# A two-layer decoder on one core: the first layer's feed-forward split by batch pairs, its weights and scratch moved, its heads made by pairs

## The chip, the cores and the metric

The kernel runs as one program on 1 core of one Trainium2 chip. The metric is device time in microseconds (us), lower is better. The time before is the median of 3 runs, 899.75 us, with 895.15 and 903.39 us as the ends. One more execution was taken by the hardware profiler; all durations below come from it.

## What is computed

The input is x of 4 batches by 256 tokens by 256 features and a context of 4 by 256 by 128. Two pre-norm decoder layers follow. Cut to what matters:

```python
x = x + L0_attn(ln(x))            # 8 query heads and 2 key/value heads of 32, rotary, unit layernorm
                                  # of q, k, v; window of 64 tokens; tanh soft cap; softmax
x = x + L0_xattn(ctx, ln(x))      # state-space scan of the context, 256 channels x 16 states,
                                  # its output gated by silu(ln(x))
x = x + L0_ffn(ln(x))             # silu(x@gate.T*gs) * (x@up.T*us) @ down.T * ds, 704 wide
x = x + L1_attn(ln(x))            # 16 query and 4 key/value heads of 128, causal
x = x + L1_xattn(ctx, ln(x))      # a second scan, gated in the same way
x = x + L1_ffn(ln(x))             # 32 experts, 6 chosen per token, and a shared expert
```

The scan is `state = state * exp(d * A) + d * u * B`, `y = sum over states of state * C`, along the 256 tokens. It depends on the context alone; only the gate at its end needs x.

## The kernel before

Tokens lie on the 128 partitions, so x is eight tiles of 128 tokens, two per batch. All arithmetic on TensorE is 32-bit except the far-mask product (L486); each 32-bit product is recorded as two instructions.

**The scan.** A scan is run for a pair of batches at a time (bp 0 or 1, two batches side by side in a row of 512). `mamba_front(l, bp, ...)` makes u, dt and du on TensorE, ScalarE and VectorE and writes the rows of B and C to DRAM (L204). `mamba_scan` is a Python generator. Each state costs: two row loads `bt` and `ct` on SyncE's queue (L232), an exponential on ScalarE into a PSUM bank (L238), `db` on GpSimd (L240), the scan instruction on VectorE (L241) and the product with ct on VectorE (L243). In layer 0 every second state is added up on TensorE (L258) and the others on GpSimd (L260), and one `next` of the generator makes two states; a pair of batches has 32 states, that is 16 steps (2 channel halves of 8). In layer 1 a step is one state number for both halves, added up on GpSimd (L250).

**Layer-0 attention.** `head0(b)` makes the normalized, rotated heads of one batch: projections (L393), rotation (L403, L409, L410), mean and square sum (L417 to L426), an inverse square root by three Newton steps in `rsqrt_steps` (L105 to L112), and the scaled heads (L433 to L440). `tail0(b, ..., states)` does scores, tanh, exp, the weighted sum and the output projection, and calls `states(2)` at two places, so that scan steps are traced between its parts.

**The order of the work.** The program is traced in Python in the order in which it is written; a scheduler then fills each engine's queue by that order as priority and by when it expects operands, buffers and PSUM banks to be free. On the chip each queue runs in order. The traced order around the change is: heads of batches 0 and 1; then for b = 0 to 3: two scan steps, head0(b+2) if there is one, tail0(b) with two and two more steps. After b = 0 the front of the second scan is traced, and the 3 MB weight `wqkv1` of layer 1 is loaded behind the last row load (L576). So 24 of the 32 steps are traced with the attention.

**Layer-0 feed-forward** comes next, in a `with` block of its own (L614 to L679): its weights downs, gw, uw and dw are loaded there (L618 to L624), into a pool that opens when the attention's pools have closed, and dw is scaled on GpSimd (L625). For each half hf (batches 0 and 1, then 2 and 3): the gates `gates_of` (L275), in the second half the rest of the scan (`states(99)`), `mamba_gate` (L286 to L294) and `ln_transposed` (L137 to L144) of each batch, all through the single PSUM bank of `pc`; then six pieces of 128 columns: gate and up products (L643), silu (L651), product (L654); then the down product (L669) and the sum into x (L677). In the second half five steps of layer 1's first scan are traced between the pieces. `mamba_front(1, hf, pf)` is traced after each half.

Before that block the mean over each head's 128 columns is taken out of wqkv1, in four groups of five heads: a reduction on VectorE (L607, L608) and two subtractions on GpSimd (L610). Layer 1's attention (from L683) opens its PSUM pools after `stage_a.close()` has given back all of layer 0's.

Two buffers matter: `tile_pool` PSUM banks are pa=1, pb=2, pc=1, psd=2, psy=1, pf=1, all eight; and ScalarE runs Silu, Softplus and Exp/Tanh with different function tables, each change being an ACT_TABLE_LOAD in the trace.

## Time and profile before

| what | value |
|---|---|
| median of 3 runs | 899.75 us (895.15 to 903.39) |
| the profiled execution | 899.26 us, of which the span is 897.5 us |
| TensorE clock granted, mean | 0.941 |
| busy share of the span | PE 90%, VectorE 66%, ScalarE 54%, GpSimd 47% |
| batch sums of layer-0 attention into x (L551) | at 95.3, 132.5, 157.5 and 185.6 us |
| last scan state of layer 0 added up (second L262 of bp 1) | 252.4 us |
| first product of layer 1 (L714) | 317.6 us |
| first expert product on the chain (L1015) | 650.6 us |

The span is 1.8 us shorter than the profiled execution's own time, and that is 0.5 us under the median. The stretches used below are: 0 to 132 us (heads, attention of batches 0 and 1), 132 to 186 (attention of batches 2 and 3), 186 to 253 (feed-forward of batches 0 and 1 beside the last 16 states), 253 to 317 (gates and feed-forward of batches 2 and 3), then layer 1.

In a list of groups the columns are line, engine, operation, output and inputs, shapes, count, then busy us and mean ns of one, then the idle time just before them and what ended it. In a table of stretches each engine has its busy us and its instruction count, then come the granted clock and the DMA share. In the chain of waits a row is start, length and what.

### The profile page before, as it was taken

The page shows a single profiled execution, that of the slowest core. Times are in us where ns is not written, and L with a number is a line of the kernel's source. Part 1 is how long each engine was busy: PE and PEld are TensorE (multiplying, and loading weights), DVE is VectorE, ACT ScalarE, POOL GpSimd, SP SyncE. Part 2 cuts the span into 40 slices and gives each one's busy share as a digit, 9 for nine tenths or more (in the row PEclk, how much of TensorE's full clock was granted, in tenths as well). Part 3 has the DMA queues.
Part 4 walks back from the last instruction along what each step waited for, and adds up shares of the span by engine and source line. Part 5 has one row for each costly group of instructions (what it writes and reads, how often), then busy time and mean ns, then how long its engine had stood idle before and what let it go on. Part 6 is the DMA issues. An engine that isn't in the chain of part 4 may idle for free.

```text
span 897.5 us, 10261 instructions
## 1 busy us (share of the span) xinstructions
PE 803.8 (90%) x3062; PEld 496.9 (55%) x3062; DVE 588.2 (66%) x1112; ACT 480.7 (54%) x1188; POOL 423.2 (47%) x427
## 2 busy tenths in 40 slices
PE   5788989978978989889898978997999999999997
PEld 2345656623433435546565745675666656666665
DVE  4897999775877668777759785788067676212121
ACT  5565545478848736746856693776333433211111
POOL 5654879865779624735635472422257751000000
PEclk9896889778986999999999999998999999999999
DMA  5545465672623400100110010000048743555542
GB/s 165 174 144 212 148 181 195 196 257 76 206 93 102 147 15 24 39 10 30 41 47 24 24 47 1 24 3 21 29 153 225 233 151 101 150 148 159 158 145 82
DMA packets 61015, 98.36 MB, mean 110 GB/s; under 512 B 6352, under 2 KB 26720, under 8 KB 60704
## 3 DMA queue, kind: packets, MB, share of 16 engines
q1 hardware_dynamic: 60080, 96.48, 34.4%
q10 hardware_dynamic: 880, 1.23, 0.4%
q8 instruction: 24, 0.39, 0.2%
q14 instruction: 31, 0.25, 0.1%
HBM read 96.24 MB, written 1.44 MB: 109 GB/s over the span
## 4 chain that ended last, share of the span: by engine, by line
PE 46%; DVE 12%; ACT 5%; POOL 3%; issue 3%; POOLq 0%; DVEq 0%; ACTq 0%
PE ps L1015 13%; PE ps L1029 12%; PE ps L883 5%; PE ps L714 4%; PE ps L868 2%; PE ps L821 2%; DVE ps L741 2%; DVE qs L734 1%; ACT sc L840 1%; DVE qr L742 1%; PE ps L748 1%; DVE h L241 1%; PE ps L669 1%; PE ps L643 1%; POOL sc L845 1%
## 5 line engine op out<-in xcount | busy, mean ns | idle before, releaser
L240 POOL TENSOR_TENSOR db<-bt,du 128x512 f32<-128x512 f32 x128 | 162.7, 1282 | 82.2 <-DVE h L241 57.0
L241 DVE TENSOR_TENSOR_SCAN h<-h,db 128x512 f32<-128x512 f32 x128 | 152.7, 1215 | 29.2 <-ACT h L238 28.1
L1015 PE MATMUL ps<-moe_xnT,w 128*128 128x512 f32 x272 | 128.9, 597 | 0.0
L1029 PE MATMUL ps<-w,hT 128*128 128x256 f32 x544 | 128.5, 379 | 0.0
L1020 DVE SCALAR_TENSOR_TENSOR hT<-ps,gr 128x512 f32<-128x512 f32 x64 | 44.1, 689 | 126.8 <-PE ps L1015 126.8
L238 ACT ACTIVATE h<-dt,negA 128x512 f32<-128x512 f32 x128 | 86.2, 689 | 73.5 <-DVE hc L243 71.2
L1029 PEld LDWEIGHTS ps<-w,hT 128*128 128x128 f32 x544 | 103.0, 190 | 40.2 <-issue 29.4
L1021 ACT ACTIVATE hT<-hT 128x512 f32<-128x512 f32 x68 | 42.8, 629 | 133.8 <-DVE hT L1020 133.6
L714 PE MATMUL ps<-wqkv,xnT 128*128 128x512 f32 x192 | 93.4, 598 | 8.0 <-DVE rq L706 5.6
L243 DVE TENSOR_TENSOR hc<-h,ct 128x512 f32<-128x512 f32 x128 | 84.8, 678 | 3.0 <-DMA ct<-bc 1.8
L250 POOL TENSOR_TENSOR y<-y,hc 128x512 f32<-128x512 f32 x64 | 80.8, 1272 | 8.3 <-DVE hc L243 6.4
L845 POOL TENSOR_TENSOR sc<-sc,rsum 128x512 f32<-128x512 f32 (+1 forms) x32 | 46.2, 1466 | 66.4 <-DVE rsum L843 66.3
L1015 PEld LDWEIGHTS ps<-moe_xnT,w 128*128 128x128 f32 x272 | 51.9, 192 | 36.5 <-issue 33.2
L707 POOL TENSOR_TENSOR rq<-rq,nhalf 128x8 f32<-128x8 f32 x20 | 33.0, 1651 | 80.9 <-DVE rq L706 80.7
L729 ACT ACTIVATE sq<-ps 128x128 f32<-128x128 f32 x160 | 42.4, 282 | 49.4 <-PE ps L714 49.4
L840 ACT ACTIVATE sc<-sc,nm 128x256 f32<-128x256 f32 (+1 forms) x128 | 56.7, 448 | 7.6 <-DVE nm L835 4.2
L883 PE MATMUL ps<-wo,oT 128*128 128x256 f32 x256 | 57.0, 381 | 0.0
L883 PEld LDWEIGHTS ps<-wo,oT 128*128 128x128 f32 x256 | 48.1, 190 | 8.9 <-ACT oT L876 2.6
L714 PEld LDWEIGHTS ps<-wqkv,xnT 128*128 128x128 f32 x192 | 32.7, 190 | 30.1 <-issue 17.5
L258 PE MATMUL ps<-hc,ident 128*128 128x512 f32 x64 | 39.9, 712 | 8.8 <-DVE hc L243 8.8
L260 POOL TENSOR_TENSOR y<-y,hc 128x512 f32<-128x512 f32 x32 | 40.8, 1274 | 4.8 <-DVE rs_t L110 2.1
L748 PE MATMUL ps<-ident,qr 128*128 128x128 f32 x160 | 28.1, 293 | 13.7 <-DVE qr L742 11.8
(206 smaller groups left out, 1450.6 us busy)
## 6 DMA issues: line engine op xcount, KB each, us to landing
bt<-bc SPq DMA_DIRECT2D x96, 256.0 KB, 3.5
ct<-bc SPq DMA_DIRECT2D x96, 256.0 KB, 3.8
w<-in_w_dram SPq DMA_DIRECT2D x64, 256.0 KB, 3.7
gr<-gt SPq DMA_DIRECT2D x64, 256.0 KB, 3.4
wqkv<-in_wqkv_dram SPq DMA_DIRECT2D x1, 3072.0 KB, 11.8
wo<-in_wo_dram SPq DMA_DIRECT2D x1, 2048.0 KB, 9.3
x<-in_x_dram SPq DMA_DIRECT2D x4, 256.0 KB, 5.1
w<-in_ws_dram SPq DMA_DIRECT2D x4, 256.0 KB, 3.9
```

What stands on the lines that cost most here:

```text
L238: nc.scalar.activation(h, dt[:, c, :], AF.Exp, scale=negA[:, a : a + 1])
L240: nc.gpsimd.tensor_mul(db, bt, du[:, c, :])
L241: nc.vector.tensor_tensor_scan(h, h, db, 0.0, ALU.mult, ALU.add)
L243: nc.vector.tensor_mul(hc, h, ct)
L250: nc.gpsimd.tensor_add(y[:, c, :], y[:, c, :], state(n, c, bt, ct))
L714: mm(pq, lhsT=xnT[:, f, c * P : (c + 1) * P], rhs=wqkv1[:, f, ch * 512 : (ch + 1) * 512], start=(f == 0), stop=(f == 1),)
L840: nc.scalar.activation(part, part, AF.Exp, bias=nm[:, qc, j : j + 1], accum_out=rsum[:, qc, j : j + 1])
L845: nc.gpsimd.tensor_mul(part, part, rsum[:, qc, :].unsqueeze(2).to_broadcast([P, 4, w]))
L883: mm(pout[:, c * 256 : (c + 1) * 256], lhsT=oTs[h // 4][:, h % 4, c * P : (c + 1) * P], rhs=wo1[:, 8 * gp + h, :], start=(h == 0), stop=(h ...
L1015: mm(ph_, lhsT=w[:, f * P : (f + 1) * P], rhs=xnT[:, f, :], start=(f == 0), stop=(f == 1))
L1020: gated.append(nc.vector.scalar_tensor_tensor(h, ph_, 0.0, g, ALU.max, ALU.mult).ins)
L1029: mm(po[t // 2][:, (t % 2) * 256 : (t % 2 + 1) * 256], lhsT=h[:, t * P : (t + 1) * P], rhs=w[:, 256:512], start=start and t % 2 == 0, stop ...
```

## The change

1. **Feed-forward as a generator.** `feed_forward(hf, room, pair, narrow)` holds the same work as before, with a `yield` after the gates, after each batch's gate and norm, after each of six pieces and after each down product: 11 pieces. `pair` and `narrow` say which PSUM banks it takes.
2. **Batches 0 and 1 beside the attention of batches 2 and 3.** Its pieces are traced two at a time with three scan steps (`both`), before each of the two batches and at the two fill places of each tail0. It takes the banks pf and pa in turn, and its scratch (sz, xnT, hT, sg) is the memory of wqkv1.
3. **Weights.** The feed-forward's weights get a pool that stands beside the attention's, and are loaded after batch 0, where wqkv1 was loaded; wqkv1 is loaded after the first half of the feed-forward has ended, as it shares the memory.
4. **Scan steps.** 2 + 3 + 3 for each of batches 0 and 1, then steps until the first scan has ended (17 in all), then `both`. The front of layer 1's first scan and conv_taps(1) are traced inside this stage.
5. **Heads by pairs.** `head0` does two batches up to the inverse square root in one set of instructions of double width; `normed(i)` makes the scaled heads of one. Some tiles go from two buffers to one.
6. **rsqrt_steps** has three instructions per Newton step, not four, everywhere.
7. **Second half.** Its narrow products go through pc and pa in turn; its gates are made at its start; the centring of wqkv1 (`centre`) is traced between its pieces, and the front of layer 1's second scan after the third pair.

```diff
         for _ in range(3):
-            nc.vector.tensor_mul(t_, r_, r_)
+            nc.vector.scalar_tensor_tensor(t_, r_, -0.5, r_, ALU.mult, ALU.mult)
             nc.vector.tensor_mul(t_, t_, v)
-            nc.vector.tensor_scalar(t_, t_, -0.5, 1.5, ALU.mult, ALU.add)
-            nc.vector.tensor_mul(r_, r_, t_)
+            nc.vector.scalar_tensor_tensor(r_, t_, 1.5, r_, ALU.add, ALU.mult)
...
+    fw = stage_a.enter_context(tc.tile_pool(name="f0w", bufs=1))
...
+    def load_ffn():
+        nc.sync.dma_start(out=downs, in_=rows[:, R_DOWNS : R_DOWNS + HID].to_broadcast([P, HID]))
+        nc.sync.dma_start(out=gw, in_=gate_in)
+        nc.sync.dma_start(out=uw, in_=up_in)
+        nc.sync.dma_start(out=dw, in_=down_in)
+        nc.gpsimd.tensor_mul(dw, dw, downs.unsqueeze(1).to_broadcast([P, NIC, HID]))
+
+    def feed_forward(hf, room, pair, narrow):
+
+        sz, xnT, hT, sg = room
+        szs = [gates_of(2 * hf + bb, sz) for bb in range(2)]
+        yield
+        for bb in range(2):
+            mamba_gate(0, 2 * hf + bb, next(narrow), szs[bb])
+            ln_transposed(2 * hf + bb, xnT[:, :, bb * S : (bb + 1) * S], next(narrow))
+            yield
+        for ic in range(NIC):
+            m = min(P, INTER - ic * P)
+            pg, pu = ps(next(pair)), ps(next(pair))
...
+            yield
+        for t2 in range(2):
+            pd = ps(next(narrow))
...
+            yield
...
-        def head0(b):
...
+        def head0(bs, *pools):
+
+            pools = itertools.cycle(pools)
+            r = ap.tile([P, 2, 2, 12, 32], F32, tag="r", name="r", bufs=1)
+            sq = ap.tile([P, 48, 32], F32, tag="sq", name="sq", bufs=1)
+            for i, b in enumerate(bs):
...
+            rs4 = rsqrt_steps(rs48, 48, bufs=2).rearrange("p (b c h) -> p b c h", b=2, c=2)
+            def normed(i):
...
         s0 = []
-        parts = [head0(0), head0(1)]
-        for b in range(B):
-            states(2)
-            if b + 2 < B:
-                parts.append(head0(b + 2))
-            tail0(b, *parts[b], states)
-            if b == 0:
-                first.append(mamba_scan(mamba_front(0, 1, pf), [psd], psy))
-            if b == 0:
-
-                with tc.issue_after(loads[-1]):
-                    nc.sync.dma_start(out=wqkv1, in_=wqkv1_in)
+        scans, banks = [], [psd]
+        normed = head0((0, 1), pa, pb, pb)
+        parts = [normed(0), normed(1)]
+        states(2)
+        tail0(0, *parts[0], lambda: states(3))
+        first.append(mamba_scan(mamba_front(0, 1, pf), [psd], psy))
+        with tc.issue_after(loads[-1]):
+            load_ffn()
+        states(2)
+        normed = head0((2, 3), pa)
+        parts.append(normed(0))
+        tail0(1, *parts[1], lambda: states(3))
+        parts.append(normed(1))
+        while not s0:
+            states(1)
+
+        room = wqkv1.rearrange("p f n -> p (f n)")
+        turn = itertools.cycle((pf, pa))
+        ffn = feed_forward(
...
+        def both():
+            states(3)
+            run(ffn, 2)
+
+        for b in (2, 3):
+            both()
+            tail0(b, *parts[b], both)
+            if b == 2:
+                conv_taps(1)
+        run(ffn)
+        scans.append(mamba_scan(mamba_front(1, 0, pf), banks))
+        nc.sync.dma_start(out=wqkv1, in_=wqkv1_in)
+        states(99)
...
-    for h in range(0, 20, 5):
+
+    def centre(h):
         hs = slice(h, h + 5)
...
-        for hf in range(2):
-            szs = [gates_of(2 * hf + bb, fp, 4) for bb in range(2)]
-            if hf == 1:
-                states(99)
...
+            itertools.cycle((pb,)),
+            itertools.cycle((pc, pa)),
+        )
+        run(ffn, 3)
+        for k in range(5):
+            run(ffn, 1 if k == 4 else 2)
+            run(scans[0], 1)
+            if k > 0:
+                centre(5 * k - 5)
+            if k == 2:
+                scans.append(mamba_scan(mamba_front(1, 1, pf), banks))
+        run(ffn)
```

## The prediction

> **What bounds the kernel now.** I read the page's forty slices first, then a table of stretches, then what the engines waited for in each, then the rows of single operations. Layer 1 is not edited except for the Newton steps, so the question is when layer 0 ends.
>
> ```profile
> PE   5788989978978989889898978997999999999997
> PEclk9896889778986999999999999998999999999999
> ```
>
> Forty slices of 22.4 us, busy tenths and granted clock. From slice 14 (317 us, the first product of layer 1) TensorE is about 90% busy at nearly full clock; before that it is as busy, but the clock dips. The last 247 us are expert products back to back, so a microsecond that layer 0 gives up is a microsecond of the end.
>
> ```profile
> 0.00:132.00 132.00, 105.81 (x422) 60.39 (x422) 111.08 (x204) 74.41 (x141) 81.46 (x104) 0.86 0.52 171
> 132.00:186.00 54.00, 50.51 (x246) 32.21 (x247) 43.73 (x65) 30.15 (x61) 45.23 (x43) 0.87 0.62 192
> 186.00:253.00 67.00, 58.17 (x148) 26.77 (x146) 49.89 (x75) 51.36 (x65) 44.79 (x48) 0.87 0.55 177
> 253.00:278.00 25.00, 14.95 (x32) 4.75 (x31) 20.66 (x37) 15.54 (x22) 18.68 (x23) 0.69 0.24 72
> 278.00:317.00 39.00, 36.70 (x102) 18.31 (x102) 22.60 (x34) 30.05 (x34) 26.73 (x31) 0.93 0.41 134
> ```
>
> Busy us of PE, weight load, VectorE, ScalarE, GpSimd in the five stretches. The first is VectorE's: 111 of 132, and nearly all of what is missing lies before 25 us. The second is TensorE's: 50.5 of 54. In the third, the feed-forward of batches 0 and 1, no engine is over 87%: this is what the change wants to fill. The fourth is a chain of latencies, TensorE 60% busy.
>
> ```profile
> POOL db L240 <- DVE h L241: 18.6, 13, 2.8
> DVE h L241 <- ACT h L238: 15.6, 10, 4.4
> ACT h L238 <- DVE hc L243: 14.7, 9, 3.3
> ACT pr L499 <- PE ps L490: 12.6, 5, 3.9
> ```
>
> The longest waits of 132 to 253 us. The scan's engines wait for each other, and VectorE (15.6 us) for an exponential that is late. ScalarE's 12.6 us for scores belong to the attention.
>
> ```profile
> L258 PE MATMUL ps<-hc,ident 128*128 128x512 f32 x38 | 23.4, 708 | 4.2 <-DVE hc L243 4.2
> ...
> L643 PE MATMUL ps<-f_xnT,gw 128*128 128x512 f32 (+1 forms) x24 | 13.1, 675 | 1.9 <-ACT f_xnT L144 1.9
> L669 PE MATMUL ps<-dw,hT 128*128 128x256 f32 (+1 forms) x46 | 12.1, 392 | 0.3 <-DVE hT L654 0.3
> L643 PE MATMUL ps<-f_xnT,uw 128*128 128x512 f32 (+1 forms) x24 | 11.3, 592 | 0.0
> ```
>
> TensorE's costliest rows of the same stretch: the feed-forward is 36.5 us (L643, L669) and has to be done by TensorE wherever it stands.
>
> ```profile
> 262.24 1.51 PE L202 MATMUL ps<-u,xproj 128*40 128x512 f32 x2 [4.65 <-DVE negA L208]
> 264.49 1.18 PE L141 MATMUL ps<-ident,xn 128*128 128x128 f32 x4 [0.74 <-ACT xn L137]
> 265.61 1.93 PE L202 MATMUL ps<-u,xproj 128*40 128x512 f32 x2
> 267.50 1.11 PE L288 MATMUL ps<-ident,yg 128*128 128x128 f32 x4
> ```
>
> TensorE in the fourth stretch: it stood 4.65 us in front of the second scan's front (L202), and the transposes of batch 3's gate (L288) came at 267.50, though their operands were written by 259.4 (VectorE's rows): the one bank of pc was still held by batch 2's transposes, copied out at 266.87 to 267.45.
>
> **First stretch (0 to 132 us, VectorE).** Out go Newton instructions. In the rows of VectorE the four heads have 4 x (1 + 12) = 52: 0.7 + 4.8 + 3.6 + 5.7 + 3.4 = 18.2 us (L105, L109 to L112), 0.35 us each; afterwards 2 x (1 + 9) = 20. At 0.35 that is 7.0 us, so 11.2 saved. Isolated rows of 128x24 take 0.18 and the dearest line averages 0.48; 20 at these make 3.6 and 9.6, so the saving is 8.6 to 14.6. The other pair instructions have twice the elements; I give them no saving (one 768-element reduction takes 0.94, of which little can be a start-up). Centring goes to the fourth and fifth stretch: L607 and L608 are 5.9 + 1.7 = 7.6 us, of which 6.4 here, and 4.9 of L610's 9.9 on GpSimd. In comes scan: 34 states are traced before batch 2 where 26 ran by 132 us. Eight at 1.22 + 0.68 are 15.2 us of VectorE; on GpSimd 8 x 1.30 + 4 x 1.27 = 15.5; on TensorE 8 instructions of L258 at 0.71 = 5.7. The weights' scaling adds 3.6 on GpSimd (L625). VectorE: 111.1 - 11.2 - 6.4 + 15.2 = 108.7; GpSimd 81.5 - 4.9 + 15.5 + 3.6 = 95.7; TensorE 111.5 of 132. The stretch keeps its end: 0 us. A pair's heads come later for the first batch of it by up to one head's VectorE work, about 12 us in the rows of 30 to 50 us, and scan steps stand ready to cover it; if they did not, +12. The best case is VectorE's 2.4. On SP's queue four weight loads (0.33 to 0.42 us of issue each, 2.2 MB) stand where one of 3 MB stood, ahead of the same row loads: 0.
>
> **Second and third together (121 us, TensorE).** TensorE's work is 50.5 + 58.2 - 5.7 = 103.0 us busy. Nothing is taken out of the feed-forward. What changes is what can fill its gaps. At the share of the attention stretch (50.51/54 = 0.935) this takes 110 us, at that of the feed-forward stretch (0.868) 118.7, without a gap 103. So -11, with -2 and -18 as bounds. I take -11: the nearest row is that of the stretch in which scan and attention already run beside each other. VectorE has 43.7 + 49.9 - 15.2 = 78 us and GpSimd 71 in it, so neither is the bound. The feed-forward's weights no longer wait for the attention's end (gw issued at 186.06, first L643 at 211.65).
>
> Each piece has one pair of banks (pf, pa), as before (pb's two): product, silu, product, then the next. Before, six pieces took 211 to 242 us. There is room for that in 110. What is queued behind: in ScalarE's queue the attention's tanh and exp stand behind each silu, and TensorE's next scores behind their bank.
>
> ```profile
> 293.39 0.02 issue
> 293.41 1.28 ACT L238
> 294.69 0.01 issue
> 294.71 0.69 ACT h L238
> ```
>
> This is the chain of the fifth stretch: a table load takes 1.28 us, and the exponential starts 0.02 us after it. A visit to silu between exponentials costs two loads and its own 0.69, 3.25 us of ScalarE. In 186 to 253 us such visits met no attention; afterwards they do. Eight are new there (six pieces, two pairs of gates; the front's two met the attention already): 8 x 3.25 = 26 us of delay in front of tanh, which costs nothing where TensorE has other work queued and all of it where it has not. ScalarE's 81.5 busy of 121 leave room, so I take 0 and keep 26 for a rival. The Trainium skill, ScalarE: Activation LUTs (What ACT_TABLE_LOAD costs), speaks against the change more strongly: a drain of about 1.38 us comes on top of the 1.28, 2.66 us for every switch. By it the eight visits would be 48 us of delay. The row shows no such drain in front of this load, which starts 0.02 us after the silu before it ended (293.39), so it is left out of the sum.
>
> **Fourth and fifth (64 us).** pc and pa in turn let batch 3's gate run beside batch 2's norm: up to 267.50 - 259.4 = 8 us. The second front moves behind three pairs of pieces: up to 4.65, of which I take 2, since other waits stand close behind. Against that, the gates of batches 2 and 3 were made ahead of the scan's end and are now made after the attention's end: norm statistics 1.1, GpSimd's four small instructions 1.4, a table load 1.28, two silus 1.2, together +5. Centring adds 7.6 us of VectorE (busy 43.3 of 64) and 9.9 of GpSimd (45.4 of 64): covered by their idle time; one L607 or L610 ahead of a link of the chain costs 1.3 to 1.5, so 0 to +6, I take +1. wqkv1 is loaded after the down products of the first half, at about 242: 11.8 us to landing, then four groups of 1.48 + 0.16 + 2 x 1.26 = 4.2: ready at 271 even one after the other, about 30 us ahead of L714. What waits behind that load on SP's queue is the rows of layer 1's scan. Sum: -8 - 2 + 5 + 1 = -4, bounds -13 and +11.
>
> **Layer 1** has the same scan steps (five before it, 14 with it). Three instructions less in each of two routings lie beside expert products: 0.
>
> **Sum**, against the profiled execution: 899.3 + 0 - 11 - 4 = 884 us; that execution is 0.5 us under the median, which I neglect.
>
> **Rivals.** *A: TensorE was the bound already.* The shares do not rise: -2 from the middle stretches, 0 at the end: 897. For it: 88% busy from 25 to 253 us (200 of 228). Against: the gaps are long single ones. *B: silu visits stall the attention (slower).* One mechanism: ScalarE's queue between scores and tanh, 132 us to the attention's end. All eight count: 884 + 26 = 910. It eats the gain from the fifth visit on and makes the kernel slower by 1% only if seven to eight stall TensorE. For it: VectorE's 15.6 us behind L238 in this stretch. Against: ScalarE itself waits 12.6 us for scores. *C: the clock as well.* In 132 to 253 it was 0.87; the same work at full clock would take 108.7 x 0.13 = 14 us less: 870. For it: dense pieces now stand among thin attention products. The Trainium skill, TensorE: Matmul & The Clock Gate (Part 1), says that sustained activity releases the throttle; but 75 to 100 us has TensorE busy 23.7 of 25 at a clock of 0.59, so being busy by the profile does not suffice, and C is no part of the forecast.
>
> **Numbers.** Chances: the forecast 0.40, C 0.14, A 0.20, B 0.26. A measurement of this kernel can tell about 1%, 9 us. Around the forecast alone: 872 (-18 in the middle, -9 at the end) to 897 (-2 and 0). The range reaches to B and C: 862 to 914. Faster by over 1% (under 890.8): C and most of the forecast, 0.52. Slower by over 1%: most of B, 0.25. Within 1%: 0.23.
>
> **What would show it.** Right: the middle stretches' sum about 11 us shorter, TensorE at 93% in it; L288 of batch 3 within 4 us of batch 2's; L714 at about 302. Wrong: idle TensorE in front of L486 or L490 behind ScalarE (B); L714 waiting for wqkv1 or its centring; the first stretch ending after 140 because the pair's heads are late; or row loads stuck behind the wqkv1 load.

## The result and the profile after

The changed kernel takes 906.85 us (median of 12 runs, 903.82 to 910.51), the kernel before in the same series 897.37 us (12 runs, 893.21 to 905.36): ratio 1.010, 95% interval 1.0069 to 1.013. It is about 1% slower; 884 us was forecast. The profiled execution has a span of 904.8 us against 897.5, and the two spans are compared below. Between L113 and L294 the line numbers of the changed kernel are one lower than before; after that: attention's add L618 (was L551), pieces L376, L384, L387 (L643, L651, L654), down products L401 and their add L409 (L669, L677), centring L706 and L709 (L607, L610), layer 1's projections L768 (L714), inverse square root of keys and queries L761 (L707), scores L875 (L821).

The forty slices of the page (22.6 us each), changed kernel:

```profile
PE   5888859789978969889988988997999999999997
PEclk9968858899989989899999999998999999999999
```

The clock's dents of before at slices 8, 9 and 13 (0.7, 0.7, 0.6) are gone (0.8, 0.9, 0.9); a new one stands at slice 6 (113 to 136 us, TensorE half busy at 0.5), where batches 2 and 3 have their heads made, and slice 15 (316 to 339, the start of layer 1) is 0.6 busy where it was 0.8. Stretches of the changed kernel, cut at its own events: batch 1's attention done, batch 2's, batch 3's, first product of the second half, first product of layer 1 (L768), first scores of layer 1 against 256 keys (L875, called the first scores below; those against 128 keys, L866, start 3.1 us earlier in both kernels). Columns are length, then busy us of PE, weight load, VectorE, ScalarE, GpSimd, then clock, DMA share, GB/s.

```profile
0.00:145.80 145.80, 113.03 (x410) 61.75 (x412) 114.39 (x178) 83.11 (x145) 94.67 (x115) 0.79 0.55 171
145.80:198.50 52.70, 45.30 (x184) 25.42 (x180) 45.24 (x70) 38.64 (x60) 39.82 (x42) 0.94 0.60 191
198.50:245.60 47.10, 44.60 (x198) 26.93 (x196) 27.95 (x42) 23.59 (x43) 20.82 (x20) 0.96 0.39 127
245.60:273.40 27.80, 20.22 (x48) 7.41 (x47) 18.40 (x38) 16.89 (x25) 17.77 (x25) 0.88 0.40 140
273.40:321.00 47.60, 42.60 (x118) 19.82 (x116) 30.31 (x41) 35.55 (x43) 35.31 (x37) 0.96 0.35 113
321.00:349.70 28.70, 23.41 (x68) 11.34 (x69) 22.39 (x49) 13.28 (x64) 15.57 (x18) 0.88 0.17 56
```

The last three of the same events in the kernel before, whose first half ends with its down products' add at 258.2:

```profile
258.20:278.00 19.80, 10.93 (x20) 3.23 (x21) 15.46 (x31) 14.85 (x21) 15.22 (x20) 0.61 0.23 67
278.00:317.50 39.50, 36.70 (x102) 18.31 (x102) 23.06 (x35) 30.05 (x34) 26.73 (x31) 0.93 0.40 133
317.50:340.80 23.30, 20.23 (x68) 9.86 (x69) 18.75 (x41) 10.69 (x59) 6.26 (x7) 1.00 0.00 1
```

So the first half ends 12.6 us earlier (245.6 for 258.2), and each of the next three stretches is longer: +8.0, +8.1 and +5.4. At the first scores the change is 8.9 us behind (349.7 for 340.8); from there both kernels need 555 to 557 us. TensorE does more in these three stretches: 20.22 + 42.60 + 23.41 = 86.2 us of products where it did 67.9, 18.4 more. Nearly all of that is the fronts of layer 1's two scans: of their 48 products (L188, L201, L210) 43 start behind the end of the first half and take 24.5 us, where it was 8 of them and 7.6 us in the kernel before: 16.9 us more.

TensorE of the changed kernel in the gate chain:

```profile
254.91 0.49 PE L287 MATMUL ps<-ident,yg 128*128 128x128 f32 x3
255.33 1.91 PE L201 MATMUL ps<-u,xproj 128*40 128x512 f32 x4
257.18 0.33 PE L287 MATMUL ps<-ident,yg 128*128 128x128 f32 x1
257.91 1.12 PE L210 MATMUL ps<-xdbl,dtproj 8*128 8x512 f32 x2 [0.41 <-ACT xdbl L202]
259.91 1.97 PE L210 MATMUL ps<-xdbl,dtproj 8*128 8x512 f32 x2 [0.88 <-ACT dt L212]
262.66 4.92 PE L188 MATMUL ps<-ctxT,taps 128*128 128x512 f32 x6 [0.78 <-ACT dt L212]
```

L201 and L210 belong to the front of layer 1's first scan, which ran between 165 and 201 us before, beside the attention; L188 of 262.66 is already the second front, whose products of this line (L189) ran mostly beside the first half's feed-forward before:

```profile
201.58 2.01 PE L189 MATMUL ps<-ctxT,taps 128*128 128x512 f32 x2
204.24 2.96 PE L189 MATMUL ps<-ctxT,taps 128*128 128x512 f32 x6
...
254.84 2.74 PE L189 MATMUL ps<-ctxT,taps 128*128 128x512 f32 x6
```

In the changed kernel a front's product stands between the transposes of batch 3's gate (L287). GpSimd there, in the same stretch as the first of these views:

```profile
258.54 5.34 POOL L709 TENSOR_TENSOR wqkv<-wqkv,wmean 128x640 f32<-128x640 f32 x4 [5.08 <-DVE wmean L707]
...
264.01 0.80 POOL L124 TENSOR_SCALAR ln_nb<-ln_mv 128x2 f32<-128x2 f32 x1
...
268.16 0.20 POOL L127 TENSOR_TENSOR ln_nb<-ln_nb,ln_rs 128x2 f32<-128x2 f32 x1
```

Four centring instructions stand ahead of batch 3's norm (L124 to L127), on which the second half's first product waits. And in layer 1's start, VectorE and GpSimd:

```profile
312.95 2.34 DVE L240 TENSOR_TENSOR_SCAN h<-h,db 128x512 f32<-128x512 f32 x2
...
316.71 2.33 DVE L240 TENSOR_TENSOR_SCAN h<-h,db 128x512 f32<-128x512 f32 x2
...
321.06 1.22 DVE L240 TENSOR_TENSOR_SCAN h<-h,db 128x512 f32<-128x512 f32 x1
...
323.17 1.22 DVE L240 TENSOR_TENSOR_SCAN h<-h,db 128x512 f32<-128x512 f32 x1
```

```profile
328.43 0.71 POOL L126 TENSOR_TENSOR ln_rs<-ln_rs,nhalf 128x2 f32<-128x2 f32 x1
329.22 0.19 POOL L127 TENSOR_TENSOR ln_nb<-ln_nb,ln_rs 128x2 f32<-128x2 f32 x1
329.37 1.26 POOL L249 TENSOR_TENSOR y<-y,hc 128x512 f32<-128x512 f32 x1
330.59 1.65 POOL L761 TENSOR_TENSOR rq<-rq,nhalf 128x8 f32<-128x8 f32 x1
```

Six scan states lie in front of the first keys; the keys' inverse square root (L761) had its operand at 327.8 and starts 2.8 us later. The kernel before has no state between 308.8 and 340.8, and its L707 follows its operand by 0.1 us:

```profile
323.07 1.64 POOL L707 TENSOR_TENSOR rq<-rq,nhalf 128x8 f32<-128x8 f32 x1 [2.96 <-DVE rq L706]
```

### The profile page after: what moved, and what is told of

Same layout as the page of the kernel before. It is cut to its first block, busy times and chain, and to the rows that moved or that the text cites. A ratio compares the mean times of both kernels' runs of the same rounds, so it can differ in the third digit from the quotient of the medians.

```text
span 904.8 us, 10214 instructions
## 1 busy us (share of the span) xinstructions
PE 804.4 (89%) x3062; PEld 496.2 (55%) x3062; DVE 578.5 (64%) x1066; ACT 479.3 (53%) x1185; POOL 423.9 (47%) x427
## 4 chain that ended last, share of the span: by engine, by line
PE 47%; DVE 11%; ACT 4%; POOL 3%; issue 2%; DMA 0%; SPq 0%; DVEq 0%; ACTq 0%; POOLq 0%
PE ps L1083 13%; PE ps L1069 12%; PE ps L937 5%; PE ps L768 5%; PE ps L922 2%; PE ps L875 2%; PE ps L376 2%; ACT sc L894 1%; DVE ps L795 1%; PE ps L802 1%; DVE qs L788 1%; DVE qr L796 1%; DVE h L240 1%; POOL sc L899 1%; POOL rq L761 1%
## 5 line engine op out<-in xcount | busy, mean ns | idle before, releaser
L239 POOL TENSOR_TENSOR db<-bt,du 128x512 f32<-128x512 f32 x128 | 164.9, 1301 | 76.1 <-DVE h L240 57.5
L768 PE MATMUL ps<-wqkv,xnT 128*128 128x512 f32 x192 | 96.1, 613 | 9.5 <-DVE rq L760 3.8
L761 POOL TENSOR_TENSOR rq<-rq,nhalf 128x8 f32<-128x8 f32 x20 | 33.0, 1652 | 73.3 <-DVE rq L760 73.2
L257 PE MATMUL ps<-hc,ident 128*128 128x512 f32 x64 | 43.4, 766 | 22.9 <-DVE hc L242 22.7
L768 PEld LDWEIGHTS ps<-wqkv,xnT 128*128 128x128 f32 x192 | 33.5, 195 | 32.6 <-issue 17.9
L802 PE MATMUL ps<-ident,qr 128*128 128x128 f32 x160 | 28.8, 299 | 15.4 <-DVE qr L796 11.7
```

The lines of the kernel that those rows point to most:

```text
L239: nc.gpsimd.tensor_mul(db, bt, du[:, c, :])
L768: mm(pq, lhsT=xnT[:, f, c * P : (c + 1) * P], rhs=wqkv1[:, f, ch * 512 : (ch + 1) * 512], start=(f == 0), stop=(f == 1),)
```

## The experiments

Theories. T: what was won in front of the second half is given back behind it by work that the change moved there; its parts are the front, the centring (T2) and the down products' bank. Rivals: Z, the pairs of heads cost it in the first stretch; B, the silu visits stall the attention. W came out of the first four runs: TensorE's work up to the second half sets its sum, so a gain in one place is work moved to another. G, that the chain of gates made after the attention lies uncovered, came with e9; S, about the start of layer 1, came last.

All runs beside the kernel before on the same chip. "First half" is the time of its last add in the profiled run (attention of batch 3 or down products, whichever is later); then come the us from there to layer 1's first product, and from there to its first scores.

| run | us | ratio to before (95%) | first half | to product | to scores |
|---|---|---|---|---|---|
| before (profile) | 897.4 | 1 | 258.2 | 59.3 | 23.3 |
| changed | 906.9 | 1.010 (1.0069 to 1.013) | 245.6 | 75.4 | 28.8 |
| e1 centring late | 912.5 | 1.0178 (1.0136 to 1.022) | 243.6 | 79.7 | 29.6 |
| e2 downs in pa | 906.4 | 1.0127 (1.0092 to 1.0162) | 243.6 | 74.4 | 28.8 |
| e3 front early | 908.3 | 1.0146 (1.0106 to 1.0186) | 260.2 | 62.9 | 23.3 |
| e4 single heads | 912.2 | 1.018 (1.0146 to 1.0214) | 248.0 | 76.3 | 27.4 |
| e5 pair early | 905.7 | 1.0109 (1.0074 to 1.0144) | 242.5 | 73.9 | 27.4 |
| e6 no centring | 902.4 | 1.0081 (1.0051 to 1.011) | 241.5 | 71.7 | 30.7 |
| e7 tanh | 911.9 | 1.0172 (1.0138 to 1.0205) | 246.7 | 73.9 | 27.4 |
| e8 before, Newton | 903.2 | 1.0075 (1.004 to 1.011) | 264.8 | 58.5 | 23.3 |
| e9 downs last | 903.2 | 1.0058 (1.0026 to 1.009) | 241.8 | 70.6 | 30.6 |
| e10 before, front late | 914.0 | 1.0182 (1.0144 to 1.0219) | 255.1 | 68.6 | 31.3 |
| e11 = e5 + e3 | 901.7 | 1.0057 (1.0026 to 1.0089) | 261.9 | 48.7 | 31.0 |
| e12 = e9 + e5 | 901.2 | 1.0046 (1.0021 to 1.007) | 241.9 | 72.3 | 30.7 |
| e13 steps later | 920.1 | 1.0242 (1.0202 to 1.0282) | 247.9 | 76.6 | 33.0 |
| e14 = e12 + e13 | 911.5 | 1.0157 (1.0111 to 1.0202) | 239.7 | 73.0 | 31.5 |
| e15 = e11 + e13 | 903.1 | 1.0081 (1.0049 to 1.0112) | 255.9 | 49.3 | 31.5 |
| e16 before, steps later | 895.8 | 0.9985 (0.9957 to 1.0013) | 249.1 | 54.8 | 23.3 |
| e17 hold | 910.0 | 1.0155 (1.0101 to 1.021) | 244.5 | 74.7 | 30.3 |
| e18 = e11 + hold | 902.3 | 1.0078 (1.0044 to 1.0112) | 263.3 | 47.1 | 30.5 |

Each profile is one execution, and such points scatter. Where the order up to there is the same (changed, e1, e2, e6, e13, e17), the profiles put the end of the first half at 241.5 to 247.9. The kernel before scatters more: e16 has the first 824 products recorded on TensorE in the same order, yet is 5.7 us earlier at 250 us (granted clock 0.98 for 0.87 between 132 and 186) and ends the first half at 249.1 for 258.2. So differences of 6 us between two profiles, and of 9 against the kernel before, mean nothing by themselves; the 12.6 us could be as little as 3.5. What follows rests on the times and on differences that several profiles repeat.

**Single moves undone.** e1:

```diff
             if k > 0:
-                centre(5 * k - 5)
+                with tc.issue_after(hts[6]): centre(5 * k - 5)
```

(`hts` collects the instructions of L387; the seventh is the second half's first.)

> The changed kernel with one edit: the centring of wqkv1 (L704 to L711) may only be issued behind the first hT (L387) of the second half. Theory T (the 7.5 us won before the second half are given back behind it, by work that was moved there): from the end of the first half's down products to the second half's first product was 27.8 us, with L706 (2.9 us) on VectorE and L709 (5.3 + 2.6 us) on GpSimd ahead of batch 3's norm; without them 22 to 24, and the time falls by 4 to 6 us, to about 902 where the changed kernel gives 907. The centring is then ready near 300, still ahead of L768 at 321. If centring covers nothing else: no new wait. Theory Z (the heads made by pairs cost it, in the first stretch) and theory B (silu visits in front of the attention) expect no change, within 1 us.

The gate chain became shorter (24.6 us from 243.6 to the first L376, for 27.8), as T2 had it, but the pieces took 37.3 us for 33.0: moved, not removed, and the kernel is slower than the changed one. T2's cure failed. e2:

```diff
-            pd = ps(next(narrow))
+            pd = ps(next(down or narrow))
...
-            itertools.cycle((pc, pa)),
+            itertools.cycle((pc, pa)), itertools.cycle((pa,)),
```

> The changed kernel with one edit: the second half's down products use the bank of pa alone, as in the kernel before; pc is left to the gates, so that layer 1's transposition bank (which lies on pc) is free early. Theory T: the transposes of batch 0's norm of layer 1 move between the two groups of down products, from 318.5 to about 308; the first product of wqkv1 (L768) follows the last down product within 11 to 12 us of its first instead of 14.6, and the first keys need 3 to 5 us less: the time falls by 4 to 7 us, to about 901. Against that, the second group waits for the add of the first (L409), up to 2 us. Theories Z and B: no change, within 1 us, or +2.

The norm's transposes did move between the down products, and nothing followed: 74.4 and 28.8. The bank is not it. e3:

```diff
             if b == 2:
                 conv_taps(1)
+                scans.append(mamba_scan(mamba_front(1, 0, pf), banks))
         run(ffn)
-        scans.append(mamba_scan(mamba_front(1, 0, pf), banks))
```

> The changed kernel with one edit: the front of layer 1's first scan is traced behind the attention of batch 2, where it stood in time in the kernel before, and not behind the first half's last piece. Theory T: the stretch behind the first half holds one front instead of two, which gives back 3 to 6 us there; in the middle stretch the front's products (8 of L188, 2 of L201, 2 of L210, some 7 us of TensorE) come back, and TensorE is about 95% busy in it, so 3 to 7 us are lost there: net -3 to +3, about 906, and what counts is that the stretch from the end of the first half to the first L768 shrinks from 75.4 to about 71. Theory Z: 0 in both. Theory B: the front's silus and softpluses are three to four more visits among tanh and exp, +5 to +10, 915.

This is the run that says most. Its stretches from batch 2's attention on:

```profile
194.50:260.20 65.70, 61.53 (x226) 33.98 (x225) 42.67 (x58) 43.66 (x66) 39.20 (x37) 0.90 0.39 130
260.20:281.20 21.00, 13.79 (x33) 4.22 (x31) 18.59 (x33) 15.69 (x22) 17.57 (x24) 0.82 0.46 185
281.20:323.10 41.90, 38.08 (x105) 18.92 (x105) 23.19 (x42) 28.42 (x34) 26.24 (x32) 0.93 0.32 107
323.10:346.40 23.30, 20.27 (x68) 9.85 (x69) 17.93 (x38) 11.11 (x60) 6.26 (x7) 1.00 0.00 1
```

With the front in its old place the stretches behind the first half are nearly those of before (21.0, 41.9, 23.3 for 19.8, 39.5, 23.3), and the first half ends at 260.2, no earlier than before (258.2). Three later runs with this edit (e11, e15, e18) put that end at 255.9 to 263.3, and all twelve with the front late, the changed kernel among them, at 239.7 to 248.0: what was won there was the front's absence. The time is not better than the changed kernel's. e4:

```diff
...
-        normed = head0((0, 1), pa, pb, pb)
-        parts = [normed(0), normed(1)]
+        parts = [head0((0,), pa, pb, pb)(0)]
+        parts.append(head0((1,), pa, pb, pb)(0))
...
-        normed = head0((2, 3), pa)
-        parts.append(normed(0))
+        parts.append(head0((2,), pa)(0))
+
         tail0(1, *parts[1], lambda: states(3))
-        parts.append(normed(1))
+        parts.append(head0((3,), pa)(0))
```

> The changed kernel with one edit: the heads are made one batch at a time again (1 head a call, the shorter Newton steps kept), the others of the pair behind the attention in front. Theory Z: batch 1's attention ends at 132 instead of 145 and the 13 us are won back at the end, 895. Theory T: the heads' delay only shifted work between the first and the middle stretch (their sum fell by 7.5), so batch 1 ends 8 to 13 us earlier, but the end of the first half moves by 0 to -4 and the time by the same: 903 to 907. Theory B: no change.

Batch 1 ends at 134.1 for 145.8, batch 2 at 196.5 for 198.5, the first half at 248.0: nothing arrives, and the time is worse. Z falls. e5 attacks the same hole from the other side:

```diff
-        states(2)
+        states(2); normed = head0((2, 3), pa)
         tail0(0, *parts[0], lambda: states(3))
...
-        normed = head0((2, 3), pa)
         parts.append(normed(0))
```

> The changed kernel with one edit: the heads of batches 2 and 3 are traced ahead of batch 0's attention instead of behind it (their last products, queries and keys, stay behind it). In the changed kernel VectorE was idle for some 29 of the first 97 us and full from 100 to 150, while TensorE was busy 2 to 3.5 us in each 5 from 110 to 135 at a clock of 0.50. Theory Z2 (the hole at 110 to 135 is lost time, whatever single heads gave): the pair's VectorE work moves into the idle first 97 us, batch 1 ends at about 134 instead of 145, the middle starts 12 us earlier with the same work, and the end comes 8 to 12 us earlier: about 897. Theory W (the sum of the stretches up to the second half is set by the work that TensorE has to do in them, and a hole in one is filled from the next): batch 1 ends 8 to 12 us earlier, the end of the first half by 0 to 4, the time falls by 0 to 4: 903 to 907.

Batch 1 ends at 123.0, 22.8 us earlier, batch 2 at 204.9, 6.4 later; the ratio is that of the changed kernel. W as expected. e6 and e7:

```diff
-            if k > 0:
-                centre(5 * k - 5)
```

> The changed kernel without the centring of wqkv1 (L705 to L711 left out altogether, so the means stay in layer 1's query and key columns): this bounds what the centring costs where it stands. Moving it behind the first hT had shortened the gate chain from 31.1 to 27.9 us and made the pieces 4.2 us longer. Theory T2 (centring is a cost of the tail wherever it is put there): chain 27 to 28, pieces 29 to 31 instead of 33, the first L768 6 to 8 us earlier, the time 6 to 8 less, about 900. If the tail's length comes from the second front and the gates alone: 0 to -2, 906.

```diff
-                s_[0:m, :], pg[0:m, :], AF.Silu, scale=par[0:m, P_GATES + ic : P_GATES + ic + 1]
+                s_[0:m, :], pg[0:m, :], AF.Silu if hf else AF.Tanh, scale=par[0:m, P_GATES + ic : P_GATES + ic + 1]
```

> The changed kernel with tanh in place of silu in the first half's six pieces (their activation is another function, so the feed-forward of batches 0 and 1 is another one): the pieces' visits beside the attention need no other table. Theory B (visits to silu stall the attention): six visits less at 3.25 us, the middle stretch up to 20 us shorter, the time 887 to 897. Theory W: ScalarE is busy 62 of 99 us there and TensorE waits for products' operands, not for it: table loads go, the end of the first half moves by 0 to -3, the time 904 to 907.

Without centring the profile reaches L768 7.8 us earlier (313.1) and the scores 5.9 earlier, but 4.1 us of that stood there at the end of the first half already, ahead of any centring; the gate chain takes 23.8 us for 27.8. The interval of the time overlaps that of the changed kernel, so the centring's cost is 0 to about 4 us (the medians are 906.9 and 902.4). Without the silu visits the first half ends at 246.7 and the time does not fall: B falls.

**Parts alone, on the kernel before.** e8 has only the shorter Newton steps:

```diff
-            nc.vector.tensor_mul(t_, r_, r_)
+            nc.vector.scalar_tensor_tensor(t_, r_, -0.5, r_, ALU.mult, ALU.mult)
             nc.vector.tensor_mul(t_, t_, v)
-            nc.vector.tensor_scalar(t_, t_, -0.5, 1.5, ALU.mult, ALU.add)
-            nc.vector.tensor_mul(r_, r_, t_)
+            nc.vector.scalar_tensor_tensor(r_, t_, 1.5, r_, ALU.add, ALU.mult)
```

> The kernel before with one part of the change alone: the Newton steps of three instructions instead of four (L105 to L112), heads still one batch at a time. 12 instructions of VectorE less in the heads, at 0.35 us 4.2 us of the VectorE-bound first stretch; 6 less in layer 1's routing. Theory W and the prediction: -4 in the first stretch, 0 to -4 at the end, 893 to 897 beside the kernel before's 897. If a scheduler's other order costs more than this: above 899.

Fewer instructions, and slower by 0.75%. Batch 3's attention ends at 187.0 for 186.3; in these two profiles about 6 us are lost between 187 and 224, with another order in the queues. TensorE's wait there in e8, then in the kernel before:

```profile
PE ps L258 <- DVE hc L243: 8.3, 2, 5.8
```

```profile
PE ps L258 <- DVE hc L243: 4.0, 2, 2.1
```

The columns are us in total, times, longest. ScalarE loads a table five times between 186 and 197 us, three times in the kernel before; an exponential and its scan product come late, and behind that product TensorE's queue holds the front's second L211 and the transposes of the first half's norm (L141). e10 has only the displaced front:

```diff
-            scans.append(mamba_scan(mamba_front(1, hf, pf), banks))
+            with tc.issue_after(downs_[-1]) if hf == 0 else nullcontext():
+                scans.append(mamba_scan(mamba_front(1, hf, pf), banks))
```

(`downs_` collects L669, so the front's products queue behind the last one of the first half.)

> The kernel before with one part of the change alone: the products of layer 1's first front (L189, L202, L211) may only be issued behind the last down product of the first half, where the change has put them by giving its bank to the pieces. Theory W (the 7.5 us won in front of the second half are this front, which went behind it): the first half's last add comes at about 249 instead of 258, the stretch from there to layer 1's first product (L714) takes about 70 instead of 59, the first scores come 3 to 8 us later, the time is 900 to 905. If the front is free to move, as the prediction took it: 896 to 898. If its absence lets the feed-forward begin earlier for good: 890.

Lost: 1.8%, more than the whole change. The first half ends 3.1 us earlier, within the scatter, L714 comes 9.3 us later from there and the scores 8.0. The second front, which uses the same bank, moved along: 46 of the 48 products of both stand behind the first half's end, 24.0 us, much as in the changed kernel. So the place of the fronts is worth more than anything the prediction summed.

**Other orders at the seam.** e9 lets the first half's down products cover the gate chain:

```diff
-            run(ffn, 2)
+            run(ffn, n_steps[-1])
...
         for b in (2, 3):
+            n_steps.append(4 - b if b > 2 else 2)
             both()
...
-        run(ffn)
-        scans.append(mamba_scan(mamba_front(1, 0, pf), banks))
-        nc.sync.dma_start(out=wqkv1, in_=wqkv1_in)
+        first_half = ffn
...
-        run(ffn, 3)
+        run(ffn, 1)
+        run(first_half)
+        scans.append(mamba_scan(mamba_front(1, 0, pf), banks))
+        nc.sync.dma_start(out=wqkv1, in_=wqkv1_in)
+        run(ffn, 2)
```

> The changed kernel with another order at the seam: one piece of the first half per visit in batch 3's attention instead of two, its two groups of down products (24 of L401, some 12 us of TensorE) traced behind the gates of batches 2 and 3, and the front of layer 1's first scan and the load of wqkv1 behind them. In the changed kernel nothing dense is left for TensorE after batch 3's attention: 27.8 us from there to the second half's first product. Theory G (the gates made after the attention are an uncovered chain): the down products cover 6 to 10 us of it, batch 3's attention ends at 232 to 238 instead of 245.6, and the first product of the second half comes 4 to 8 us earlier: 899 to 903. Theory W (TensorE's work up to the second half is what counts, whatever its order): the down products only stand where idle time stood before and the front's products are pushed further into the pieces: 0 to -3, 904 to 907. Centring follows the later load of wqkv1 (landing near 262) and lies among the pieces, as where it was moved behind the first hT: +2 to +4 against both.

Batch 3's attention ends at 234.7 and the first product of the second half comes at 261.7 for 273.4, the earliest so far; the ratio falls to 1.0058, an interval that still touches the changed kernel's. G holds in the profile, and part of it is lost again in the pieces and at the scores (30.6). e11 is e5 and e3 together, e12 is e9 and e5:

> The changed kernel with two of the edits above together: the heads of batches 2 and 3 ahead of batch 0's attention, and layer 1's first front behind batch 2's attention. Single they gave 905.7 and 908.3 where the changed kernel gives 906.9. Theory W: the idle time of VectorE in the first 97 us is used, and the front lies where TensorE has room again: the first half ends at 252 to 256, 66 us to the first L768 as with the front alone, 900 to 905. If holes only move (the clock at 0.50 after each): 906 to 908.

> The changed kernel with the order at the seam of the run with the down products last, and the heads of batches 2 and 3 ahead of batch 0's attention. Theory G: both gains add, 897 to 902. Theory W: 903 to 907.

Both are near 901.5 and still behind the kernel before. e11 has the first product of layer 1 at 310.6, 7 us ahead of the kernel before, and loses all of it before the scores (31.0 for 23.3), with six scan states in front of the keys as in the changed kernel.

**The start of layer 1.** e13 leaves the second half's five steps of layer 1's scan to layer 1; e14 and e15 add this to e12 and e11, e16 to the kernel before:

```diff
-            run(scans[0], 1)
...
-        DONE, EARLY = 5, 19
+        DONE, EARLY = 0, 19
```

> The changed kernel with one edit: no step of layer 1's scan is traced in the second half (L729 goes, DONE 0 instead of 5), and layer 1's attention takes 19 steps instead of 14. Theory S (the five steps, which need the front that was displaced, are late and stand in GpSimd's and VectorE's queues ahead of the first keys: L761 had its operand at 327.8 and started at 330.6, behind the scan's L249 and batch 1's norm, where it started at once in the kernel before): the stretch from the first L768 to the first scores shrinks from 28.8 to 23 to 24 us, the pieces and down products get 2 to 4 us shorter as well, and the time falls by 6 to 9, to 898 to 901; the ten states cost layer 1 0 to 3 of it. If the front itself or the clock is the cause: 28 us as before, 905 to 907. If layer 1 has no room for ten states more (19 us of VectorE, 25 of GpSimd in 300): above 908.

> The run with the down products last and the early pair (901.2), with the five steps left to layer 1 as well. Theory S: from L768 to the first scores 23 to 24 instead of 30.7 us, the time 893 to 896, below the kernel before's 897. Otherwise 899 to 903.

> The run with the early pair and the front behind batch 2's attention (901.7), with the five steps left to layer 1 as well. Theory S: from L768 to the first scores 23 to 24 instead of 31.0 us, the time 894 to 897. Otherwise 900 to 903.

> Control: the kernel before with the five steps of layer 1's scan left to layer 1 (none traced in the second half). Theory S: there the front is early, the steps lie beside the pieces and are done when the keys begin (23.3 us from L714 to the first scores already), so there is little to gain: 895 to 898. If the steps cost the same wherever they are: 889 to 891. If layer 1 has no room for them: above 900.

S's expectations missed: e13 and e14 are slower than without the edit (1.0242 for 1.010, 1.0157 for 1.0046), e15 stays where it was, and e16 is no different from the kernel before (0.9985), though its profile reaches the first scores 13.6 us earlier, 9.1 of them won before the first half's end and so ahead of the edit. The pieces do get shorter (e13: 26.5 us for 33.0), but the attention's own first steps, which nothing holds back, take the vacated place in front of the keys (33.0 us to the scores). And five steps more in layer 1 cost 8.9 us from the first scores to the last attention's add, 318.7 for 309.8 in e16 against the kernel before, 1.8 us a step: layer 1 has little room. e17 and e18 hold these early states behind the queries:

```diff
-                with tc.issue_after(pace[-3]) if len(pace) > 2 else nullcontext():
+                with tc.issue_after(pace[-3] if len(pace) > 2 else rqs[-1]):
```

(`rqs` collects L761.)

> The changed kernel with one edit: the scan's states of layer 1's attention steps 0 to 2 (L1146) may be issued on GpSimd only behind the inverse square root (L761) of the queries traced last; the five steps of the second half stay. Theory S (these states, late because their front was displaced, stand ahead of the first keys): no state between the first L768 and the first scores, which follow it after 23 to 25 us instead of 28.8; btT and batch 0's norm come 1 to 2 us earlier; the time falls by 4 to 7, to 900 to 903; the states cost layer 1 0 to 3 of it. If the start of layer 1 is slow for another reason (the clock after idle time, L768's operands): 28 us as before, 906 to 908.

> The run with the early pair and the front behind batch 2's attention (901.7; it reached the first L768 at 310.6, 7 us ahead of the kernel before, and its first scores at 341.6, 0.8 behind it), with the same hold on the states of attention steps 0 to 2. Theory S: 23 to 25 us from L768 to the first scores instead of 31.0, and 894 to 897, the first version not behind the kernel before's 897. Otherwise 900 to 903.

TensorE and GpSimd of e17:

```profile
319.22 3.67 PE L768 MATMUL ps<-wqkv,xnT 128*128 128x512 f32 x8 [1.05 <-DVE ln_mv L121]
324.68 1.96 PE L768 MATMUL ps<-wqkv,xnT 128*128 128x512 f32 x4 [1.79 <-DVE rq L760]
...
328.33 1.10 PE L768 MATMUL ps<-wqkv,xnT 128*128 128x512 f32 x2 [0.36 <-DVE qr L796]
...
338.21 0.66 PE L802 MATMUL ps<-ident,qr 128*128 128x128 f32 x4 [3.03 <-DVE qr L796]
```

```profile
324.69 1.64 POOL L761 TENSOR_TENSOR rq<-rq,nhalf 128x8 f32<-128x8 f32 x1 [3.74 <-DVE rq L760]
333.44 1.64 POOL L761 TENSOR_TENSOR rq<-rq,nhalf 128x8 f32<-128x8 f32 x1 [7.10 <-DVE rq L760]
335.04 2.48 POOL L239 TENSOR_TENSOR db<-bt,du 128x512 f32<-128x512 f32 x2
```

The keys now run as in the kernel before: the third group of L768 comes 9.1 us after the first (before 317.55 to 326.71, 9.2; changed 320.96 to 334.24, 13.3). So the states were what delayed the keys: S holds as to the cause. TensorE's clock (0.88 in the stretch for 1.00 before) is not it: the first eight products of L768 take 5.37 us in the changed kernel and 3.67 in e1, e6 and e9, whose third group still comes 14.3 to 14.4 us after the first. But behind the keys the held states meet the queries: L802 waits 3.03 us, and the scores still take 30.3 us. The work was moved a second time, not hidden; S's gain did not come.

## Why the prediction was wrong, point by point

- **First stretch (0).** The named wrong sign came, batch 1 ending at 145.8 instead of 133; the bound of +12 was right in size. Its meaning was not: e4 and e5 take the delay away, and the end of the kernel does not move. The shorter Newton steps, counted there as VectorE time saved, cost 0.75% when made alone (e8), through the order in the queues, a price that no row of before could give. One reading was wrong as well: nearly all of VectorE's idle time was put before 25 us, while the rows have 12.4 us there and 8.0 between 25 and 95.
- **Middle (-11).** Batch 3's attention and the first half's feed-forward are done at 245.6; the two stretches' end moved by 7.4 us from 253 (12.6 from the first half's own end). TensorE's share did not rise to the sum's 93.5%: from the end of batch 1's attention to the end of the first half it is 90% before (112.7 of 125.0 us) and 90% after (89.9 of 99.8); only the last 47 us show 95%. So rival A's premise held over the whole, and its price for the middle was about right: with the front where it had been, the first half ends no earlier (e3). The sum counted the feed-forward's products and overlooked that the front of layer 1's first scan, at 165 to 201 us in the same trace, would lose its bank (pf, now the pieces') and its early place.
- **The end (-4): the step that failed.** 64 us should have become 60; from the first half's end to layer 1's first product it is 75.4 for 59.3. Of its terms, "The second front moves behind three pairs of pieces ... I take 2" took a saving for the move of one front. Both fronts were displaced, and their products came into this stretch as 16.9 us more of TensorE, a cost to which the sum gave no term (e10 prices the displacement at 1.8% in the kernel before). Of the up to 8 us for pc and pa in turn 3.0 came: the gates' sums of batches 2 and 3 (L293) end 7.8 us apart for 10.8, and batch 3's L287 stand at 254.9 to 257.2, 7.4 us behind batch 2's at 247.5, with a front's products between them. The +5 for gates made after the attention is of the right kind: the chain is 27.8 us for 19.8, and covering it (e9) brought the second half's first product forward by 11.7. Centring, +1 within 0 to +6: L709 ahead of batch 3's norm; 0 to about 4 by e6. The bound of -13 was also too low by the sum's own terms: it left out the +5.
- **Layer 1 (0).** Right from the first scores on (555.1 for 556.7 us); wrong for its first 23.3 us, which became 28.8. Scan states in front of the keys and among keys and queries bring that: every profile with none there has 23.3 (before, e3, e8, e16), every one with them 27.4 to 33.0. The displaced front makes them late in the changed kernel, and e3 takes them away; but e11, e15 and e18 have the first front early and states there all the same.
- **Rivals.** B, the one that ended on the slower side, gave nearly the right time (910) by luck, for a reason that e7 refutes: ScalarE's table loads between 130 and 260 us fall from 18 to 6 and the time does not. A table load stays at 1.28 us with the next activation 0.01 to 0.06 us behind it where its operand is there (257.88 and 262.62 us), without the drain that The Trainium skill, ScalarE: Activation LUTs (What ACT_TABLE_LOAD costs), adds. C happened in part (clock 0.87 to 0.94 and 0.96 in the middle, 0.79 for 0.86 in the first stretch) and changed nothing at the end. "L714 waiting for wqkv1": no, it waits for batch 0's norm.

What stays open: no single edit brings back the 1%, and putting the first front back (e3) does not either, since the middle then takes its time again. The largest steps down (e9, e11, e12) leave 0.5%, and edits that should cost nothing move the time by 0.7 to 0.8% (e7 against the changed kernel, e8, by the order of the queues, against the one before), so the remaining microseconds cannot be split among the gates, the centring and the late states. That some tiles of layer 0's attention went from two buffers to one was not tried apart.

## What to carry to other kernels

Before crediting a gain to "filled gaps", list everything that lies in the stretch, also work of the next stage that a scheduler pulled forward there, and ask whether the change leaves it its bank and its place; here the microseconds won were this work. Count a stretch's products before and after (67.9 and 86.2 us): if the sum behind the gain has grown, the gain was borrowed. And take more than one profile of a kernel before reading a few microseconds out of it: the same order gave ends 9 us apart. And undo a delay before blaming it: batch 1's 12 us, plain in the profile, were worth nothing.

## What was not expected of the hardware

TensorE, changed kernel, in windows of 5 us:

```profile
110.00:115.00 5.00, 3.30 (x26) 3.11 (x23) 5.00 (x6) 3.62 (x9) 3.05 (x3) 0.83 0.87 206
125.00:130.00 5.00, 2.03 (x2) 0.45 (x2) 5.00 (x8) 1.31 (x2) 3.64 (x4) 0.50 0.60 209
135.00:140.00 5.00, 5.00 (x17) 2.78 (x17) 4.96 (x9) 2.61 (x5) 5.00 (x6) 0.50 0.62 181
140.00:145.00 5.00, 5.00 (x26) 3.63 (x27) 4.98 (x6) 2.68 (x7) 4.91 (x5) 0.94 0.68 199
```

After a stretch at 2 to 3.5 us of 5, the clock stays at 0.50 through five more busy microseconds, and a 128x512 product takes 2.07 us there (L257 at 131.28) instead of 1.02 (L188 at 242.03; each product is two recorded instructions). The Trainium skill, TensorE: Matmul & The Clock Gate (Part 1), gives about 3.4 us of sustained activity for the release, counted in a window that runs freely of the kernel; two such windows, 6.8 us by an estimate from the page's figure, would still cover this row. They do not cover e4:

```profile
95.00:100.00 5.00, 5.00 (x14) 2.35 (x13) 4.41 (x6) 4.51 (x8) 4.07 (x4) 0.50 0.64 169
100.00:105.00 5.00, 5.00 (x14) 2.82 (x14) 0.35 (x1) 3.90 (x9) 1.79 (x2) 0.50 0.39 147
```

Here TensorE is shown as busy for 10 us and the clock stays at 0.50; the row decides. What sets it apart from a release after 3.4 us, no run shows.
